# A transformer block on one core: which engine takes decays and normalisations, and how far a planner looks into its chains

## The chip, the core and the metric

One core of a Trainium2 chip. TensorE (PE) does matmuls and transposes, VectorE (DVE), ScalarE (ACT) and GpSimd (POOL) work on elements, SyncE (SP) issues DMAs. Each engine takes its instructions in the order in which the program has them. The metric is the device time of one launch in microseconds, the median of several executions. All data are float32; a matmul of the program stands in the trace as two MATMUL records, a transpose as one.

## The reference

Eight sequences (batches) of 512 tokens, width 256, go through one block of four residual steps:

```python
x = x + attn_a(layernorm(x))     # 16 heads of 16, keys and values through a latent of 64, rope,
                                 # softmax(q k / 4 + log decay(distance)) v, + 0.2 sigmoid(q mean k) mean v, Wo
x = x + ffn(layernorm(x))        # relu(x W1 + b1) W2 + b2, inner width 1024
x = x + attn_b(layernorm(x))     # (q k * gamma^(i-j) for i >= j) v, no softmax, one head of 256
x = x + ffn(layernorm(x))        # the same weights again
```

A layernorm is `(x - mean) / sqrt(var + 1e-5)` over 256 elements. The first attention's log decay is applied as a factor: `exp(score - max) * dec_a`, and the sum over keys comes out of the same matmul by a column of ones.

## The kernel before

**Items and steps.** The first attention is cut into 32 items (8 batches x 4 groups of 4 heads); each has 8 score tiles `s` (two heads, 128 queries x 512 keys each) and 8 probability tiles `t` (the same transposed). A step n of the planner issues on TensorE the four matmuls of `s_n` and `t_{n-12}`. `reduce_item` then takes the row maxima of `s` on VectorE (`mr`, TENSOR_REDUCE 128x1024); once an item's 8 are there, `shift` puts them, negated, into `qT` (`mx`, a transpose, an ACT copy and a DMA). `soft_item` makes `p` from `t`: Exp on ScalarE, then two multiplications with `dec_a` (the decays, TENSOR_TENSOR 128x512) on GpSimd or VectorE, as `pooled[n]` says. `pv_item` multiplies `p` with the values (`pv`).

**Banks.** `s` and `t` share two PSUM buffers of two banks (`ps_sc`), so `s_{n+1}` waits for the `mr` of `s_n`, and `t` for the Exp of the `t` before it. In early steps (`EARLY`) `t` may take two of the three single banks (`ps_m`), which everything else uses too; these tiles are named `t0_n`, `t1_n`.

**The other work.** Everything else is cut into `Unit`s in chains: `front1`/`front2` (layernorm `a`, latent `lat`, keys `k`, queries `q`, values `v`, gate `ga`, mean rows `mv`, `me`), `post_units` (division of the numerators by the sums), `rest(b)` (`wo`; layernorm `f`; feed-forward `hx2` and `x2`; layernorm `r`; second attention `b`, `bv`, `bs`, `bo`; layernorm `g`; feed-forward `hx4` and `x4`), and `rest_last` for the last batch, in two chains of half a batch. A name such as `hx2_7_0_1` is that unit's tile: batch 7, column block 0, second half.

**Layernorms.** `ln_units` makes three units for each half (two tiles of 128 tokens): `stats` (`st`, `mv` on VectorE; `ve`, the variance plus eps, and `rstd`, a power, on GpSimd), `norm` (`xn = (x - mean) * rstd`, two TENSOR_SCALAR 128x256 on VectorE; for `f` and `g` also two additions of the bias `b2` to `x` on GpSimd), and `turn` (four transposes `tr_`, then an ACT copy to `xT`).

**Division.** `post_units(i, fast)`: for groups 0 and 1, and for all groups of batches `fast` to 6, it goes by DMA: `num` copied out of PSUM, rows to `aT` and sums to `sums`, a reciprocal, a DMA to DRAM and a broadcast DMA back (`rec`), then `aT * rec` on VectorE. Otherwise groups 2 and 3 are transposed (`num`), divided, and turned back (`aT`). `wo` needs `aT`.

**The order.** All instructions are pinned to the order in which Python emits them. `plan(reserve, later, early, fast, lead, bias, emit)` walks through steps and chains with clocks of its own for PE, DVE, ACT and POOL. It runs once for each of 144 rules (lists `RESERVES` to `BIASES`) with `emit=False`; the rule with the least planned end is run again with `emit=True`. In its main loop, units without TensorE work (`pe` 0) are issued as soon as they are ready, but only from the head of a chain; the best TensorE unit at the head of a chain is taken if the next step must wait or if its credit allows; `values` issues `pv`.

```python
            prob_at[i] = clock["POOL" if pooled[i] else "DVE"] = on if pooled[i] else own
...
    cost = {r: plan(*r) for r in rules}
    plan(*min(rules, key=cost.get), emit=True)
```

In `step`, the matmuls, Exp and decays are emitted ahead of the lines that set `pooled[i]`; `soft_item` thus reads what an earlier call of `plan` left in `pooled`, that of the last rule in the list. The rule that this kernel's planner takes is (reserve 90000, later 0, early 8, fast 3, lead 3000, bias 3000), which is the last of the list.

Of the kernel before, what the change touches and what calls it, by code (L numbers as in the profile page):

```python
# [9 lines left out]
F32 = mybir.dt.float32  # L10
AF = mybir.ActivationFunctionType
ALU = mybir.AluOpType
# [23 lines left out]
def tile_kernel(  # L36
# [217 lines left out]
    RESERVES, LATERS, EARLIER, FAST = (75000, 90000), (-45000, -30000, 0), (0, 8), (1, 3)  # L254
    LEADS, BIASES = (0, 1500, 3000), (0, 3000)
    NS = 8 * NI
    LAG, FILL, BONUS = 12, 300, 300
    PER = 8 * NG
    EARLY = PER + 2
# [47 lines left out]
    class Unit:  # L307
        def __init__(self, fn, pe=0, then=(), after=(), step=0, gives=None, needs=(), bank=True):
            self.fn, self.pe, self.then, self.after, self.step = fn, pe, then, list(after), step
            self.gives, self.needs, self.banks, self.done = gives, needs, int(bank) if pe > 0 else 0, None  # L310
            self.takes = self.frees = False
            self.holds, self.lets, self.behind = [], [], []


# [13 lines left out]
    def ln_units(get, name, pool, bias=None):  # L328
        s = {}

        def stats(h):
            xt = get()
            if h == 0:
                s["st"] = rs.tile([P, NT, 6], F32, tag="st", name=f"st_{name}")
                s["mv"] = rs.tile([P, NT, 2], F32, tag="mv", name=f"mv_{name}")
                s["ve"] = rs.tile([P, NT], F32, tag="ve", name=f"ve_{name}")
                s["rstd"] = rs.tile([P, NT], F32, tag="rstd", name=f"rstd_{name}")
            two = slice(2 * h, 2 * h + 2)
            for t in (2 * h, 2 * h + 1):
                dve.bn_stats(s["st"][:, t, :], xt[:, t, :])  # L340
            for t in (2 * h, 2 * h + 1):
                dve.bn_aggr(s["mv"][:, t, :], s["st"][:, t, :])
            gps.tensor_scalar(s["ve"][:, two], s["mv"][:, two, 1], EPS, None, ALU.add)
            gps.tensor_tensor(s["rstd"][:, two], s["ve"][:, two], half[:, two], ALU.pow)

        def norm(h):
            xt = get()
            if h == 0:
                s["xn"] = rs.tile([P, NT, D], F32, tag="xn", name=f"xn_{name}")
                s["xT"] = pool.tile([P, NC, T], F32, tag="xT", bufs=1 if pool is fr else 2, name=f"xT_{name}")  # L350
            for t in (2 * h, 2 * h + 1):
                dve.tensor_scalar(
                    s["xn"][:, t, :], xt[:, t, :], s["mv"][:, t, 0:1], s["rstd"][:, t : t + 1],
                    ALU.subtract, ALU.mult,
                )
# [11 lines left out]
        u = []  # L367
        for h in range(2):
            a = Unit(lambda h=h: stats(h), then=(("DVE", 1200), ("POOL", 1450)))
            b = Unit(lambda h=h: norm(h), then=(("DVE", 1100),) + (() if bias is None else (("POOL", 1550, "aside"),)), after=[a])  # L370
            u.append([a, b, Unit(lambda h=h: turn(h), 520, (("ACT", 600),), after=[b])])
        Hold("st", 2, u[0][0], u[1][1]), Hold("xn", 2, u[0][1], u[1][2])
        return s, u

# [665 lines left out]
    def plan(reserve, later, early, fast, lead, bias, emit=False):  # L1040
# [26 lines left out]

        def issue(u):
            t = start_of(u)
            if emit:  # L1070
# [7 lines left out]
            for e, ns, *aside in u.then:  # L1078
# [85 lines left out]
        def step(t):  # L1164
# [11 lines left out]
            shape[0] = "S"  # L1176
            at_ += 1070
            clock["PE"] = at_
            if emit:
                mms, after = [], []  # L1180
                if s is not None:
                    ps, m = score_item(s)
                    mms += m
                    after.append((reduce_item, s, ps))
                for i in ts:
                    ps, m = prob_item(i)
                    mms += m
                    after.append((soft_item, i, ps))
                for o, l, r in mms:
                    mm(o, l, r)  # L1190
                for f, k, ps in after:
                    f(k, ps)
# [6 lines left out]
            for i in ts:  # L1199
                if spare[i]:  # L1200
                    for e in range(2):
                        clock["ACT"] = max(clock["ACT"], at_ + 100) + 650
                        banks.popleft()
                        banks.append(clock["ACT"])
                else:
                    clock["ACT"] = max(clock["ACT"], at_ + 100) + 1090
                    sc.popleft()
                    sc.append(clock["ACT"])

                on = max(clock["ACT"] + 60, clock["POOL"]) + 2750  # L1210
                own = max(clock["ACT"] + 60, clock["DVE"]) + (1650 if i < EARLY else 1500)
                pooled[i] = on <= own + (lead if i < EARLY else bias)
                prob_at[i] = clock["POOL" if pooled[i] else "DVE"] = on if pooled[i] else own

        def backlog():
# [48 lines left out]
        while t < LAST or any(chains) or posts or shifts or valued[0] < NS:  # L1264
            while True:
                ready = [
                    c for c in [shifts, posts] + chains
                    if c and not c[0].pe and c[0].step <= t and start_of(c[0]) is not None
                    and start_of(c[0]) <= clock["PE"] + 300
                ]  # L1270
                if not ready:
                    break
                for c in ready:
                    if start_of(c[0]) is not None:
                        issue(c.pop(0))
            s_step = step_start(t) if t < LAST else None

            idle = t >= LAST or s_step is None or s_step > clock["PE"] + 400
            free = t < 2 * PER or backlog() > reserve
            best = None  # L1280
            for rank, c in enumerate([shifts, posts] + chains):
                if not c or not c[0].pe or c[0].step > t:
# [4 lines left out]
                s = start_of(c[0])  # L1287
                if s is None:
                    continue

# [1 line left out]
                if t >= LAST:  # L1292
                    key = (max(s - (BONUS if c is last_two[0] or c is last_two[1] else 0), clock["PE"] + 50), -rank)
                if best is None or key < best[0]:
                    best = (key, c, s)


            full = t < LAST and steps[t][1] and steps[t][1][-1] - valued[0] >= PB
# [9 lines left out]
            elif one is not None and one <= soon and wait > FILL and not other:  # L1308
                k = 1
            if k and other and shape[0] == "S":  # L1310
                credit -= best[1][0].pe
                issue(best[1].pop(0))
                continue
            if k and (full or t < LAST or values_start(k) <= soon):
                values(k)
# [2 lines left out]
            if best is not None and not take:  # L1318
                soon = clock["PE"] + 50
                take = (best[1] is posts or best[1] is shifts or credit > 0) and best[2] <= max(soon, s_step)  # L1320
                take = take or idle and best[2] <= soon or best[2] + best[1][0].pe <= s_step
            if take and best is None:

                if valued[0] < NS:
# [7 lines left out]
                issue(c.pop(0))  # L1332
            elif take:
                if best[1] is not posts and best[1] is not shifts:
                    credit -= best[1][0].pe
                issue(best[1].pop(0))
            else:
                step(t)
                t += 1
# [118 lines left out]
```

## Time and profile before

| | |
|---|---|
| median of 3 runs | 1280.24 us (1279.64 to 1280.58) |
| the profiled execution | 1284.98 us; span from first to last instruction 1283.2 us |
| mean granted TensorE clock in it | 0.985 |
| VectorE: `mr`, 256 | busy 312.3 us, mean 1222 ns |
| VectorE: `xn_g` 28, `xn_f` 32, `xn_r` 32, `xn_a` 32 | 30.2, 29.3, 25.0, 20.4 us; mean 1118, 955, 820, 677 ns |
| GpSimd: `ve_f` 16 / `rstd_f` 16 (the others alike) | mean 250 ns / 736 ns |
| GpSimd: bias additions `x<-x,b` 60 | busy 45.1 us, mean 772 ns |
| ScalarE: `h_x` 128x512 with a few 128x256, 128 | minimum 474, median 687 ns |
| ScalarE: `rs<-rc` 128x512 from SBUF, 16 | median 621 ns |
| TensorE: `num` 32 / `aT` 16 transposes | busy 5.2 us / 2.5 us |

In the page, a busy time is the union of a group's instructions and the mean is that of one. "Idle before" is the time in which the engine stood still ahead of the group, with what ended it. In the windows view each stretch has its width, the busy time and number of instructions of PE, PEld (weight loads), DVE, ACT and POOL, the granted TensorE clock (1.00 is full), and the DMA share and rate. In the waits, three numbers follow a pair: total us, times, longest us. In the timeline a row begins with start and duration in us, and a bracket gives idle time before it and what ended it.

### The profile page before, as it was taken

The page shows a single profiled execution, that of the slowest core. Times are in us where ns is not written, and L with a number is a line of the kernel's source. Part 1 is how long each engine was busy: PE and PEld are TensorE (multiplying, and loading weights), DVE is VectorE, ACT ScalarE, POOL GpSimd, SP SyncE. Part 2 cuts the span into 40 slices and gives each one's busy share as a digit, 9 for nine tenths or more (in the row PEclk, how much of TensorE's full clock was granted, in tenths as well). Part 3 has the DMA queues.
Part 4 walks back from the last instruction along what each step waited for, and adds up shares of the span by engine and source line. Part 5 has one row for each costly group of instructions (what it writes and reads, how often), then busy time and mean ns, then how long its engine had stood idle before and what let it go on. Part 6 is the DMA issues. An engine that isn't in the chain of part 4 may idle for free.

```text
span 1283.2 us, 16000 instructions
## 1 busy us (share of the span) xinstructions
PE 1229.3 (96%) x6196; PEld 632.7 (49%) x6196; DVE 662.4 (52%) x989; ACT 464.3 (36%) x672; POOL 758.7 (59%) x747
## 2 busy tenths in 40 slices
PE   7988999989999999998999999999999999998997
PEld 5423345334535544354443644535543654376686
DVE  4667754775455675445644476435644364333121
ACT  2245443434353333432334234343334233512311
POOL 4379765777587675774667566675667465812000
PEclk9989999999999999998999999999999999998998
DMA  5401010001000100020000200011000100000000
GB/s 133 133 12 41 17 39 1 14 17 35 22 13 7 45 6 14 6 64 22 5 9 13 57 22 4 16 37 32 1 14 5 31 5 1 14 17 1 1 17 17
DMA packets 30872, 30.82 MB, mean 24 GB/s; under 512 B 12721, under 2 KB 22194, under 8 KB 30516
## 3 DMA queue, kind: packets, MB, share of 16 engines
q1 hardware_dynamic: 29884, 29.01, 8.3%
q8 instruction: 49, 0.80, 0.3%
q10 hardware_dynamic: 912, 0.79, 0.2%
q14 instruction: 27, 0.22, 0.1%
HBM read 13.39 MB, written 4.39 MB: 14 GB/s over the span
## 4 chain that ended last, share of the span: by engine, by line
PE 88%; DVE 7%; DMA 1%; issue 1%; POOL 1%; ACT 1%; SPq 0%; DVEq 0%; ACTq 0%
PE s L203 19%; PE x L203 18%; PE hx L203 18%; PE pv L203 8%; PE wo L203 3%; PE bs L203 3%; PE bo L203 3%; DVE mr L69 3%; PE b L203 2%; PE bv L203 2%; PE q L203 2%; PE t L203 2%; DMA wv_sb<-in_wv_dram 1%; PE warm L203 1%; PE lat L203 1%
## 5 line engine op out<-in xcount | busy, mean ns | idle before, releaser
L69 POOL TENSOR_TENSOR p<-p,dec_a 128x512 f32<-128x512 f32 x466 | 587.8, 1286 | 280.6 <-ACT p L69 280.3
L69 DVE TENSOR_REDUCE mr<-s 128x2 f32<-128x1024 f32 x256 | 312.3, 1222 | 288.1 <-PE t L203 266.6
L69 ACT ACTIVATE p<-t 128x1024 f32<-128x1024 f32 (+1 forms) x282 | 263.3, 945 | 417.8 <-PE t L203 407.6
L203 PE MATMUL s<-kT,qT 32*128 32x512 f32 x1024 | 291.8, 644 | 19.8 <-DVE mr L69 19.4
L203 PE MATMUL t<-qT,kT 32*128 32x512 f32 x1024 | 288.1, 644 | 1.6 <-DVE mv_a L69 1.6
L203 PE MATMUL x<-w_sb,h_x 128*128 128x256 f32 x960 | 221.6, 384 | 0.0
L203 PEld LDWEIGHTS x<-w_sb,h_x 128*128 128x128 f32 x960 | 178.0, 190 | 58.9 <-issue 33.6
L203 PEld LDWEIGHTS s<-kT,qT 32*128 32x128 f32 x1024 | 77.9, 184 | 161.8 <-DVE mr L69 68.6
L203 PE MATMUL pv<-p,va 128*32 128x512 f32 x1024 | 129.9, 608 | 0.0
L69 ACT ACTIVATE h_x<-hx,vec 128x512 f32<-128x512 f32 (+1 forms) x128 | 84.6, 661 | 120.3 <-PE hx L203 116.5
L203 PE MATMUL hx<-xT_g,w_sb 128*128 128x512 f32 (+1 forms) x288 | 124.6, 570 | 0.7 <-ACT xT_g L69 0.7
L203 PE MATMUL hx<-xT_f,w_sb 128*128 128x512 f32 (+1 forms) x288 | 123.2, 564 | 1.2 <-ACT xT_f L69 1.0
L69 DVE TENSOR_TENSOR x<-x,x 128x256 f32<-128x256 f32 x60 | 25.4, 424 | 164.6 <-PE x L203 159.6
L203 PEld LDWEIGHTS hx<-xT_g,w_sb 128*128 128x128 f32 x288 | 52.5, 195 | 66.3 <-issue 62.4
L203 PEld LDWEIGHTS t<-qT,kT 32*128 32x128 f32 x1024 | 77.8, 183 | 11.7 <-ACT p L69 3.9
L203 PEld LDWEIGHTS hx<-xT_f,w_sb 128*128 128x128 f32 x288 | 51.9, 194 | 60.1 <-issue 46.3
L69 POOL TENSOR_SCALAR ve_g<-mv_g 128x2 f32<-128x2 f32 x16 | 3.6, 226 | 101.6 <-DVE mv_g L69 101.6
L203 PEld LDWEIGHTS pv<-p,va 128*32 128x32 f32 x1024 | 25.0, 109 | 75.2 <-issue 54.5
L69 DVE TENSOR_TENSOR p<-p,dec_a 128x512 f32<-128x512 f32 x46 | 43.6, 985 | 19.3 <-ACT p L69 19.2
L69 POOL TENSOR_TENSOR x<-x,b 128x256 f32<-128x256 f32 x60 | 45.1, 772 | 6.6 <-DVE xn_g L69 4.6
L69 POOL TENSOR_TENSOR rc<-rc,rs 128x512 f32<-128x512 f32 x30 | 38.5, 1306 | 9.1 <-DVE rs L69 9.1
L203 PE MATMUL wo<-wo_sb,aT 128*128 128x256 f32 x128 | 36.5, 405 | 5.2 <-DVE aT L69 4.3
(164 smaller groups left out, 1126.1 us busy)
## 6 DMA issues: line engine op xcount, KB each, us to landing
kT<-rc SPq DMA_DIRECT2D x64, 64.0 KB
qT<-rc SPq DMA_DIRECT2D x60, 64.0 KB
x<-in_x_dram SPq DMA_DIRECT2D x7, 512.0 KB
out_dram<-x SPq DMA_DIRECT2D x28, 128.0 KB
aT<-num SPq DMA_DIRECT2D x96, 32.0 KB
rec<-d_rec SPq DMA_DIRECT2D x12, 256.0 KB
w_sb<-in_w_dram SPq DMA_DIRECT2D x2, 1024.0 KB
x<-in_x_dram SPq DMA_DIRECT2D x2, 256.0 KB
```

The source lines that it names most:

```text
L69: ins = f(*a, **k)
L203: tc.keep_in_program_order(nc.tensor.matmul(o, lhsT=l, rhs=r, start=start, stop=stop))
```

## The change

Four things are changed.

1. In `step`, the emission moves behind the lines that set `pooled[i]`, so that the decays are emitted on the engine that the same run of `plan` chose. The planned time of a pair of decays on VectorE is 2300 ns where GpSimd is busy for more than 300 ns beyond their start, and 1500 otherwise (before: 1650 early, 1500 later).
2. Units of layernorms (`stats` and `norm`) are marked `norm`. Those without TensorE work may be issued from any of the first `AHEAD = 6` places of a chain, and `product_of` finds a chain's first TensorE unit past marked ones.
3. `norm` runs on ScalarE (`on_act`: an activation Identity with scale `rstd` and bias `nm = -mean * rstd`, with `nm` a scalar_tensor_tensor 128x2 on VectorE) or on VectorE as before, by the planner's clocks when the unit is issued.
4. `ve` moves from GpSimd to VectorE; the planned times of `stats` and `norm` change; the second half's units of a layernorm stay behind the first half's (`behind`).

```diff
+    AHEAD = 6
...
-            gps.tensor_scalar(s["ve"][:, two], s["mv"][:, two, 1], EPS, None, ALU.add)
+            dve.tensor_scalar(s["ve"][:, two], s["mv"][:, two, 1], EPS, None, ALU.add)
...
+            if b[h].on_act:
+                dve.scalar_tensor_tensor(
+                    s["nm"][:, two], s["mv"][:, two, 0], -1.0, s["rstd"][:, two], ALU.mult, ALU.mult
+                )
             for t in (2 * h, 2 * h + 1):
...
+                if b[h].on_act:
+                    act.activation(
+                        s["xn"][:, t, :], xt[:, t, :], AF.Identity, bias=s["nm"][:, t : t + 1],
+                        scale=s["rstd"][:, t : t + 1],
+                    )
+                else:
+                    dve.tensor_scalar(
...
+            def choose(t, clock):
+                d = max(t, clock["DVE"])
+                slow = clock["POOL"] > d + 200
+                b[h].on_act = max(d + 300, clock["ACT"]) + 1300 < d + (2300 if slow else 1000)
+                return ((("DVE", 300), ("ACT", 1200)) if b[h].on_act else (("DVE", 2200 if slow else 1000),)) + more
...
-            a = Unit(lambda h=h: stats(h), then=(("DVE", 1200), ("POOL", 1450)))
-            b = Unit(lambda h=h: norm(h), then=(("DVE", 1100),) + (() if bias is None else (("POOL", 1550, "aside"),)), after=[a])
-            u.append([a, b, Unit(lambda h=h: turn(h), 520, (("ACT", 600),), after=[b])])
+            a = Unit(lambda h=h: stats(h), then=(("DVE", 1280), ("POOL", 950)))
+            b.append(Unit(lambda h=h: norm(h), then=normalised(h), after=[a]))
+            u.append([a, b[h], Unit(lambda h=h: turn(h), 520, (("ACT", 600),), after=[b[h]])])
+        for h in range(2):
+            u[h][0].norm = u[h][1].norm = True
+        for one, two in zip(*u):
+            two.behind.append(one)
...
-                own = max(clock["ACT"] + 60, clock["DVE"]) + (1650 if i < EARLY else 1500)
+                own = max(clock["ACT"] + 60, clock["DVE"])
+                own += 2300 if clock["POOL"] > own + 300 else 1500
                 pooled[i] = on <= own + (lead if i < EARLY else bias)
                 prob_at[i] = clock["POOL" if pooled[i] else "DVE"] = on if pooled[i] else own
+            if emit:
...
+                for f, k, ps in after:
+                    f(k, ps)
...
+        def product_of(c):
+
+            for u in c[:AHEAD]:
+                if u.pe:
+                    return u if u.step <= t else None
+                if not u.norm:
+                    return None
+            return None
...
                 ready = [
-                    c for c in [shifts, posts] + chains
-                    if c and not c[0].pe and c[0].step <= t and start_of(c[0]) is not None
-                    and start_of(c[0]) <= clock["PE"] + 300
+                    (c, u) for c in [shifts, posts] + chains for u in c[:AHEAD]
+                    if not u.pe and (u is c[0] or u.norm) and u.step <= t and start_of(u) is not None
+                    and start_of(u) <= clock["PE"] + 300
                 ]
```

The planner of the changed kernel takes the rule (reserve 90000, later 0, early 8, fast 1, lead 1500, bias 3000). In the two built programs these counts differ:

| engine, instruction | before | after |
|---|---|---|
| GpSimd / VectorE: half decays `p` | 466 / 46 | 482 / 30 |
| VectorE / ScalarE: `xn` | 128 / 0 | 52 / 76 |
| VectorE: `nm` | 0 | 38 |
| GpSimd / VectorE: `ve` | 64 / 0 | 0 / 64 |
| TensorE: transposes `num` / `aT` | 32 / 16 | 16 / 8 |
| TensorE: `warm` matmuls on the identity | 78 | 76 |
| SyncE: DMAs of the division (`aT`, `sums`, `d_rec`, `rec`) | 144 | 168 |

More of the change, by code (lines that the diff above doesn't have):

```diff
@@ L310, in __init__ @@
             self.gives, self.needs, self.banks, self.done = gives, needs, int(bank) if pe > 0 else 0, None
-            self.takes = self.frees = False
+            self.on_act = False
+            self.takes = self.frees = self.norm = False
             self.holds, self.lets, self.behind = [], [], []
@@ L337, in stats @@
                 s["rstd"] = rs.tile([P, NT], F32, tag="rstd", name=f"rstd_{name}")
+                s["nm"] = rs.tile([P, NT], F32, tag="nm", name=f"nm_{name}")
             two = slice(2 * h, 2 * h + 2)
@@ L350, in norm @@
                 s["xT"] = pool.tile([P, NC, T], F32, tag="xT", bufs=1 if pool is fr else 2, name=f"xT_{name}")
-            for t in (2 * h, 2 * h + 1):
[L352 to L355, printed above, removed]
+            two = slice(2 * h, 2 * h + 2)
+            if b[h].on_act:
+                dve.scalar_tensor_tensor(
+                    s["nm"][:, two], s["mv"][:, two, 0], -1.0, s["rstd"][:, two], ALU.mult, ALU.mult
+                )
+            for t in (2 * h, 2 * h + 1):
+                if b[h].on_act:
[5 more added lines that the diff above has]
+                    dve.tensor_scalar(
+                        s["xn"][:, t, :], xt[:, t, :], s["mv"][:, t, 0:1], s["rstd"][:, t : t + 1],
+                        ALU.subtract, ALU.mult,
+                    )
             if bias is not None:
@@ L365, in turn, with normalised @@
             act.copy(s["xT"][:, :, 2 * h * P : (2 * h + 2) * P], ps.rearrange("p (c t) -> p c t", c=NC))
-        u = []
-        for h in range(2):
-            a = Unit(lambda h=h: stats(h), then=(("DVE", 1200), ("POOL", 1450)))
-            b = Unit(lambda h=h: norm(h), then=(("DVE", 1100),) + (() if bias is None else (("POOL", 1550, "aside"),)), after=[a])
-            u.append([a, b, Unit(lambda h=h: turn(h), 520, (("ACT", 600),), after=[b])])
+        u, b = [], []
+        more = () if bias is None else (("POOL", 1550, "aside"),)
+        def normalised(h):
+            def choose(t, clock):
[3 more added lines that the diff above has]
+                return ((("DVE", 300), ("ACT", 1200)) if b[h].on_act else (("DVE", 2200 if slow else 1000),)) + more
+            return choose
+        for h in range(2):
+            a = Unit(lambda h=h: stats(h), then=(("DVE", 1280), ("POOL", 950)))
[5 more added lines that the diff above has]
+            two.behind.append(one)
         Hold("st", 2, u[0][0], u[1][1]), Hold("xn", 2, u[0][1], u[1][2])
@@ L1069, in issue @@
             t = start_of(u)
+            then = u.then(t + 100, clock) if callable(u.then) else u.then
             if emit:
@@ L1077, in issue @@
             t += 100
-            for e, ns, *aside in u.then:
+            for e, ns, *aside in then:
                 if e is None:
@@ L1178, in step @@
             clock["PE"] = at_
[L1179 to L1192, printed above, removed]
             if s is not None:
@@ L1210, in step @@
                 on = max(clock["ACT"] + 60, clock["POOL"]) + 2750
-                own = max(clock["ACT"] + 60, clock["DVE"]) + (1650 if i < EARLY else 1500)
+                own = max(clock["ACT"] + 60, clock["DVE"])
+                own += 2300 if clock["POOL"] > own + 300 else 1500
                 pooled[i] = on <= own + (lead if i < EARLY else bias)
                 prob_at[i] = clock["POOL" if pooled[i] else "DVE"] = on if pooled[i] else own
+            if emit:
+                mms, after = [], []
+                if s is not None:
+                    ps, m = score_item(s)
+                    mms += m
+                    after.append((reduce_item, s, ps))
+                for i in ts:
+                    ps, m = prob_item(i)
+                    mms += m
+                    after.append((soft_item, i, ps))
+                for o, l, r in mms:
+                    mm(o, l, r)
+                for f, k, ps in after:
+                    f(k, ps)
         def backlog():
@@ L1272, in plan @@
                     break
-                for c in ready:
-                    if start_of(c[0]) is not None:
-                        issue(c.pop(0))
+                for c, u in ready:
+                    if (u is c[0] or u.norm) and start_of(u) is not None:
+                        c.remove(u)
+                        issue(u)
             s_step = step_start(t) if t < LAST else None
@@ L1281, in plan @@
             for rank, c in enumerate([shifts, posts] + chains):
-                if not c or not c[0].pe or c[0].step > t:
+                u = product_of(c)
+                if u is None:
                     continue
@@ L1286, in plan @@
                     continue
-                s = start_of(c[0])
+                s = start_of(u)
                 if s is None:
@@ L1294, in plan @@
                 if best is None or key < best[0]:
-                    best = (key, c, s)
+                    best = (key, c, s, u)
             full = t < LAST and steps[t][1] and steps[t][1][-1] - valued[0] >= PB
@@ L1310, in plan @@
             if k and other and shape[0] == "S":
-                credit -= best[1][0].pe
-                issue(best[1].pop(0))
+                credit -= best[3].pe
+                best[1].remove(best[3])
+                issue(best[3])
                 continue
@@ L1320, in plan @@
                 take = (best[1] is posts or best[1] is shifts or credit > 0) and best[2] <= max(soon, s_step)
-                take = take or idle and best[2] <= soon or best[2] + best[1][0].pe <= s_step
+                take = take or idle and best[2] <= soon or best[2] + best[3].pe <= s_step
             if take and best is None:
@@ L1334, in plan @@
                 if best[1] is not posts and best[1] is not shifts:
-                    credit -= best[1][0].pe
-                issue(best[1].pop(0))
+                    credit -= best[3].pe
+                best[1].remove(best[3])
+                issue(best[3])
             else:
```

## The prediction

> **What bounds the kernel now.** I read the page's busy shares and chain first, then three stages in the windows view.
>
> ```profile
> PE 1229.3 (96%) x6196; PEld 632.7 (49%) x6196; DVE 662.4 (52%) x989; ACT 464.3 (36%) x672; POOL 758.7 (59%) x747
> ...
> PE 88%; DVE 7%; DMA 1%; issue 1%; POOL 1%; ACT 1%; SPq 0%; DVEq 0%; ACTq 0%
> ```
> ```profile
> 33.40:182.70 149.30, 137.47 (x759) 54.49 (x762) 109.22 (x138) 61.07 (x114) 106.21 (x99) 0.95 0.17 51
> 182.70:1157.80 975.10, 953.22 (x4806) 468.96 (x4800) 512.27 (x746) 367.07 (x484) 622.00 (x589) 1.00 0.07 18
> 1157.80:1280.20 122.40, 113.84 (x483) 91.25 (x482) 25.53 (x78) 27.25 (x53) 16.03 (x28) 0.94 0.03 8
> ```
> TensorE is the bound: the first figure after each width is its busy time. What can be won is its idle time, 11.8 us early (149.30 - 137.47), 21.9 us in the middle, 8.6 us in the tail, and what the granted clock (next to the 0.17, 0.07 and 0.03) costs. The mean clock of 0.985 is a loss of 19 us. Then I asked what TensorE waited for, and where.
>
> ```profile
> PE s L203 <- DVE mr L69: 19.4, 21, 2.0
> PE wo L203 <- DVE aT L69: 4.3, 2, 3.4
> ```
> ```profile
> 105.61 0.70 PE L203 MATMUL s<-kT,qT 32*128 32x512 f32 x2 [1.31 <-DVE mr L69]
> ...
> 583.42 1.22 PE L203 MATMUL wo<-wo_sb,aT 128*128 128x256 f32 x2 [3.40 <-DVE aT L69]
> ...
> 1164.35 0.78 PE L206 MATMUL tr_g<-ident,xn_g 128*128 128x128 f32 x4 [1.20 <-DVE xn_g L69]
> 1167.55 1.14 PE L206 MATMUL tr_f<-ident,xn_f 128*128 128x128 f32 x4 [2.42 <-DVE xn_f L69]
> ...
> 1261.85 1.23 PE L206 MATMUL tr_g<-ident,xn_g 128*128 128x128 f32 x4 [2.94 <-DVE xn_g L69]
> ```
> ```profile
> 582.28:589.11 6.83, 5.69 (x13) 4.54 (x14) 2.10 (x5) 0.00 (x0) 0.00 (x0) 0.50 0.00 0
> 1165.96:1172.79 6.83, 4.51 (x12) 3.43 (x13) 4.05 (x13) 1.06 (x2) 6.58 (x12) 0.50 0.00 0
> 1261.53:1268.36 6.83, 5.83 (x15) 4.39 (x16) 0.59 (x2) 1.54 (x3) 1.42 (x2) 0.50 0.00 0
> ```
> Each of the three long waits is followed by 6.83 us at clock 0.50, so each costs up to 3.4 us again.
>
> **The decays.** Nothing is repaired for the kernel before: the rule its planner takes is the last of its list, so the engines left by the last cost run are its own. The order of the built programs shows the new one taking its own rule with a lead of 1500: 482 half decays on GpSimd for 466, 30 on VectorE for 46.
>
> ```profile
> L69 POOL TENSOR_TENSOR p<-p,dec_a 128x512 f32<-128x512 f32 x466 | 587.8, 1286 | 280.6 <-ACT p L69 280.3
> ...
> L69 DVE TENSOR_TENSOR p<-p,dec_a 128x512 f32<-128x512 f32 x46 | 43.6, 985 | 19.3 <-ACT p L69 19.2
> ```
> GpSimd gets 16 x 1.286 = 21 us and loses 64 adds x 0.25 = 16 us: 759 becomes 764, no bound. VectorE loses 16 x 0.985 = 16 us.
>
> **The normalisations.** 76 of 128 `xn` go to ScalarE (the four large groups, 124 of them, are busy 105 us on VectorE, 0.85 each).
>
> ```profile
> L69 DVE TENSOR_SCALAR xn_f<-x,mv_f,rstd_f x32: 380/1118/1443, 169.5 to 1169.5; 128x256 f32<-128x256 f32 x32
> ...
> L69 DVE TENSOR_SCALAR ret<-ret,bb x7: 231/873/1346, 255.2 to 1148.4; 128x4 f32<-128x4 f32 x7
> ```
> The first row (minimum, median, maximum) is 0.4 us when GpSimd is quiet and 1.35 us beside it. The second is the nearest row for the moved add (128x2): 64 x 0.23 to 0.87 = 15 to 56 us; GpSimd works in 59% of the span, so I take 64 x (0.23 + 0.59 x 0.64) = 39. The new `nm` (38) lies between the 0.15 us of the 128x2 `mv_a` and the same 0.87; I take 0.15, the row of its own size and operation: 6 us. VectorE: -65 - 16 + 39 + 6 = -36 us of 662. On ScalarE an `xn` lies between 0.41 us (two thirds of the 0.621 us that a 128x512 from SBUF takes) and 0.475 us (128x256 `h_x`): 31 to 36 us on 464. Neither is the bound, and TensorE gains only where such a step ends its wait. Queued behind the new waits are: on VectorE, behind an `nm` that waits for `rstd`, the next `mr`, and behind that `s`; on ScalarE, behind an `xn` that waits for its `nm`, the Exp and evacuations, and behind them `t` and the banks. The old `xn` waited for `rstd` on VectorE in the same place, 3.2 + 1.5 + 0.9 = 5.6 us in all (the groups of `xn_f`, `xn_a`, `xn_r`), so `rstd` is mostly there in time, and I cost these waits within the small ones below. In waiting beside GpSimd alone, 76 x (0.85 - 0.41) = 33 us go and 64 x 0.59 x 0.64 = 24 us come.
>
> By the Trainium skill, SBUF — State Buffer, Who interferes with whom, a VectorE instruction with two SBUF inputs is shut out by a GpSimd one that reads SBUF: `nm`, which reads `mv` and `rstd`, would then wait too, where the `mv_a` row, with an input from PSUM, did not. No row has so small a one with both in SBUF; the second rival prices it.
>
> **Deeper look and new order.** With AHEAD = 6 a chain's statistics and normalisations may be issued before the work ahead of them. What came of it is read off the order of both programs and priced by rows.
>
> *Transposes.* The planner now takes FAST 1 for 3, so batches 1 and 2 divide by DMA in all groups: 16 `num` and 8 `aT` transposes go, at 5.2/32 and 2.5/16 us busy each: -3.8 us. SP gets 24 more issues; the waiter behind them is `wo`, next.
>
> *`wo` after the DMA division.* From the last `pv` of batches 3 to 6 to the end of the multiply the trace shows 28.2, 21.1, 21.8 and 23.8 us; in the old order 21 to 31 us of TensorE work lie between, and batches 3 and 6 paid 3.40 and 0.89 us. In the new order 25 to 41 us lie between (durations by block). I take no wait: -4.3 us, and -3.4 us for the half clock at 582. If the cover goes (batches 2 and 6 have 25 us), 3 us return each.
>
> *Steps back to back.* With no work between two steps the next `s` waits for `mr`. Of 15 such pairs the 6 whose `t` has its own banks paid 0.0, the 9 others 1.22 to 1.96 us, 12.4 in all. The new order has 6 of the dear kind (8.2 us) and 11 of the other: -4.2 us. Runs of three now stand early (steps 27 to 29, 41 to 43), where VectorE and GpSimd are busy 109 and 106 of 149 us, so I give the five added pairs half of 1.31: +3.3 us (0 to 6.5).
>
> *Tail.* The old order has only `wo` ahead of `tr_g6`, `tr_f7`, and nothing ahead of `tr_g7_1`: 0.24 + 1.20 + 2.42 + 0.73 + 0.24 + 2.94 + 0.68 = 8.45 us idle. The new one puts `tr_r6_1`, two `b_6` and `bv_6` (4.8 us) ahead of `tr_f7`, and six `hx4_6` (10 us) ahead of `tr_g7`; from the add to the first `xn` it takes 0.69 + 0.74 + 0.30 + 0.22 + 0.71 + 0.41 = 3.1 us, so both are hidden. New is `tr_r7`, behind `x2_7_3` with only the two `tr_g6` (0.9 us) ahead: on VectorE its first half's `nm` stands behind the last add and the second half's statistics, 0.42 + 1.4 + 0.15, then ScalarE's first `xn` 0.45 and hops of 0.1 to 0.2: 2.6 - 0.9 = 1.7 us, and 0.4 more till the second half's `xn`. New is also `aT_31`: behind `x2_6_3` VectorE does its add, two `xn` and the division, 0.42 + 0.82 + 0.25 + 0.43 = 1.9 us and hops, against 0.9 us of transposes: 1.2 us. With `wo`'s 0.24: -8.45 + 3.5 = -4.9 us.
>
> *Clock in the tail.* -2 x 3.4; half windows followed 1.6 to 2.6 us idle within some 3.4 us, and did not follow 1.3 to 1.7 us, so `tr_r7` makes one or none: +1.7. Another elsewhere: +1.7. Sum -3.4 us.
>
> The Trainium skill, TensorE: Matmul & The Clock Gate, Why this matters for your kernels, allows gaps up to about 3 us. Here 2.0 us idle in two pieces ahead of 1165.96 were enough, so the measurement decides. By the page the 1.7 us for `tr_r7` would drop out.
>
> *Small waits.* The middle keeps 21.9 - 7.8 (pairs) - 4.3 = 9.8 us of waits below 1.7 us. A new order draws them anew: a `pv` whose decays stand on GpSimd behind bias adds (1.5 us) and `rstd` (0.7 us) may be late, and on ScalarE an Exp now stands behind an `xn`. Between nothing and another 9.8 + 5 us, I give +6.
>
> **Sum.** -3.8 - 4.3 - 3.4 - 4.2 + 3.3 - 4.9 - 3.4 + 6 = -14.7; taken as -14. The profiled run took 1284.98 us (span 1283.2 and 1.8 around it), 4.7 us over the median of 1280.24; the difference carries over: 1266 us.
>
> **Rivals.** *Given back in the draw* (15%): the small waits cost 9 to 17 us and the early pairs their full 6.5. For: early, both helpers are some 72% busy. Against: the middle loses 2% of its time in all. -14 + 3..11 + 3: 1272 to 1280 us, at the middle 1276.
> *`nm` held* (8%): if each `nm` waits as the 128x4 row does, 38 x (0.87 - 0.23) = 24 us come on VectorE; with a third of them ahead of an `mr` that TensorE waits for, -14 + 8 = -6: 1274 us. Against: it needs GpSimd busy each time.
> *ScalarE's queue held* (14%), the other side: an `xn` there waits for `rstd`, behind a pair of decays on GpSimd (2.57 us); all Exp behind it wait, `t` keeps its buffer, TensorE stops. 38 halves x 2.57 = 98 us; -14 + 98 x share passes zero at one in seven; at one in four it is +10: 1290 us. Against: the 5.6 us above.
> *No effect of the choice* (inside the forecast): had `on_act` not been taken the order would still differ; 76 `xn` on ScalarE in the program rule it out.
> *More* (6%): few new waits, no half clock: -24, 1256 us.
>
> **Numbers.** Forecast 57% (1258 to 1272), more 6%, given back 15% (8 faster, 7 the same), `nm` 8%, queue 14%. Measurement of this kernel tells about 0.2%, 2.6 us. Faster 0.79, same 0.07, slower 0.14. The range 1256 to 1284 leaves out half of "more" and most of "queue".
>
> **What would show it.** Right: `tr_g7` and `wo` of all DMA batches without wait, no 0.50 window near 1160 and 1250 but at most one by `tr_r7`, six dear pairs, `num` x16, `xn` on ScalarE near 0.41 to 0.48 us, `ve` on VectorE between 0.23 and 0.9. Wrong: PE busy falls by 4 us but idle stays at 50; Exp behind `xn` with ScalarE idle for GpSimd's `rstd`; `pv` waiting for GpSimd's `p` by over 10 us.

## The result, and the profile after

| | before | after |
|---|---|---|
| median of 4 runs | 1280.41 us (1279.64 to 1284.29) | 1267.56 us (1266.34 to 1269.20) |
| the profiled execution, its span | 1284.98, 1283.2 | 1267.68, 1265.9 |
| mean granted clock in it | 0.985 | 0.995 |

The ratio is 0.9888 (0.9870 to 0.9907): 12.85 us less. The two profiled executions differ by 17.3 us, because that of before lies 4.6 us over its median and that of after 0.1.

The busy shares and the chain of the page after:

```profile
PE 1225.4 (97%) x6168; PEld 628.8 (50%) x6168; DVE 615.4 (49%) x995; ACT 499.4 (39%) x746; POOL 763.6 (60%) x699
...
PE 88%; DVE 6%; POOL 2%; DMA 2%; ACT 1%; issue 1%; SPq 0%; ACTq 0%; DVEq 0%
```

TensorE is still the bound. Its idle time, span less busy, is 1265.9 - 1225.4 = 40.5 us against 53.9. VectorE has lost 47 us, ScalarE has gained 35. The windows view by stage (width, then busy time and count of PE, PEld, DVE, ACT, POOL, granted clock, DMA share, rate):

```profile
32.43:180.50 148.07, 136.94 (x749) 55.80 (x749) 108.38 (x135) 62.00 (x118) 105.67 (x93) 0.99 0.17 51
180.50:1134.30 953.80, 937.79 (x4722) 454.51 (x4720) 459.07 (x733) 397.46 (x547) 629.02 (x556) 1.00 0.07 20
1134.30:1262.90 128.60, 125.83 (x547) 100.66 (x546) 32.44 (x97) 30.91 (x60) 14.81 (x21) 0.99 0.02 8
```

Idle is 11.1 us early (before 11.8), 16.0 in the middle (21.9) and 2.8 in the tail (8.6). The clock early is 0.99 for 0.95 and in the tail 0.99 for 0.94. TensorE's waits, with total, times and longest in us:

```profile
PE s L203 <- DVE mr L69: 17.0, 22, 2.1
...
PE s L203 <- ACT p L69: 2.4, 1, 2.4
PE tr_f L206 <- ACT xn_f L69: 2.4, 4, 1.2
PE tr_r L206 <- ACT xn_r L69: 1.6, 2, 1.4
...
PE wo L203 <- ACT aT L69: 0.2, 1, 0.2
```

The waits of `wo` for the division (`DVE aT`, 4.3 us) and of `tr_g` for `xn_g` are gone. The places in the timeline that answer to those shown of before:

```profile
98.69 0.70 PE L203 MATMUL s<-kT,qT 32*128 32x512 f32 x2 [1.31 <-DVE mr L69]
...
580.07 1.13 PE L203 MATMUL wo<-wo_sb,aT 128*128 128x256 f32 x4
...
1153.37 0.60 PE L206 MATMUL tr_f<-ident,xn_f 128*128 128x128 f32 x4
...
1187.42 0.33 PE L206 MATMUL tr_r<-ident,xn_r 128*128 128x128 f32 x1 [1.42 <-ACT xn_r L69]
...
1220.21 1.04 PE L206 MATMUL tr_g<-ident,xn_g 128*128 128x128 f32 x8
```

A pair of steps back to back still costs 1.31 us where the second `s` has to wait for `mr` (below, a dear pair; a cheap one is a pair whose `t` has banks of its own). `wo`, `tr_f` and `tr_g` start without a bracket, that is without a wait; `tr_r7` waits as forecast. One window of half clock follows it (the second line below). The first line follows a step that waited 2.1 us for `mr`; a wait of 2.4 us at 469.6 brought none. Of the three windows of 6.83 us that the prediction showed none is left:

```profile
1042.34:1045.75 3.41, 3.41 (x21) 1.01 (x13) 2.57 (x4) 2.00 (x3) 2.73 (x4) 0.50 0.00 0
1189.12:1192.54 3.42, 3.40 (x8) 2.78 (x9) 0.00 (x0) 0.93 (x2) 0.00 (x0) 0.51 0.00 0
```

All windows of half clock together are 37.6 us long before and 13.6 us after. The new and moved operations (minimum, median, maximum in ns, first and last start):

```profile
L69 ACT ACTIVATE xn_f<-x,nm_f,rstd_f x28: 585/593/612, 176.0 to 1144.1; 128x256 f32<-128x256 f32 x28
...
L69 DVE SCALAR_TENSOR_TENSOR nm_f<-mv_f,rstd_f x14: 146/152/1221, 175.8 to 1142.4; 128x2 f32<-128x2 f32 x14
```
```profile
L69 DVE TENSOR_SCALAR ve_f<-mv_f x16: 168/374/1237, 172.4 to 1142.3; 128x2 f32<-128x2 f32 x16
```
```profile
L69 POOL TENSOR_TENSOR p<-p,dec_a 128x512 f32<-128x512 f32 x482 | 610.0, 1290 | 296.5 <-ACT p L69 290.1
...
L69 DVE TENSOR_TENSOR p<-p,dec_a 128x512 f32<-128x512 f32 x30 | 35.7, 1227 | 18.1 <-ACT p L69 18.1
```

An `xn` on ScalarE takes 593 ns whatever runs beside it; the two small ones on VectorE vary by a factor of seven or eight.

### The profile page after: what moved, and what is told of

Its sections match the earlier page's. It is cut to its first block, busy times and chain, and to the rows that moved or that the text cites. A ratio compares the mean times of both kernels' runs of the same rounds, so it can differ in the third digit from the quotient of the medians.

```text
span 1265.9 us, 15939 instructions
## 1 busy us (share of the span) xinstructions
PE 1225.4 (97%) x6168; PEld 628.8 (50%) x6168; DVE 615.4 (49%) x995; ACT 499.4 (39%) x746; POOL 763.6 (60%) x699
## 4 chain that ended last, share of the span: by engine, by line
PE 88%; DVE 6%; POOL 2%; DMA 2%; ACT 1%; issue 1%; SPq 0%; ACTq 0%; DVEq 0%
PE hx L203 19%; PE s L203 18%; PE x L203 18%; PE pv L203 8%; PE wo L203 3%; PE bs L203 3%; PE bo L203 3%; DVE mr L69 3%; PE b L203 2%; PE bv L203 2%; PE q L203 2%; POOL p L69 2%; PE t L203 2%; PE warm L203 1%; PE lat L203 1%; PE ga L203 1%
## 5 line engine op out<-in xcount | busy, mean ns | idle before, releaser
L69 POOL TENSOR_TENSOR p<-p,dec_a 128x512 f32<-128x512 f32 x482 | 610.0, 1290 | 296.5 <-ACT p L69 290.1
L203 PE MATMUL pv<-p,va 128*32 128x512 f32 x1024 | 132.8, 608 | 1.6 <-ACT num L69 0.7
L203 PE MATMUL hx<-xT_g,w_sb 128*128 128x512 f32 (+1 forms) x288 | 122.0, 560 | 0.0
L203 PEld LDWEIGHTS t<-qT,kT 32*128 32x128 f32 x1024 | 78.6, 183 | 14.2 <-ACT p L69 5.4
L69 POOL TENSOR_TENSOR x<-x,b 128x256 f32<-128x256 f32 x60 | 43.9, 754 | 14.7 <-DVE xn_g L69 11.6
L69 DVE TENSOR_TENSOR p<-p,dec_a 128x512 f32<-128x512 f32 x30 | 35.7, 1227 | 18.1 <-ACT p L69 18.1
L69 POOL TENSOR_TENSOR rstd_g<-ve_g,half 128x2 f32<-128x2 f32 x16 | 11.3, 704 | 54.0 <-DVE ve_g L69 53.8
L69 ACT COPY num<-pv 128x512 f32<-128x512 f32 x32 | 18.7, 585 | 57.9 <-PE pv L203 53.4
```

Source lines behind the costliest of these rows:

```text
L69: ins = f(*a, **k)
L203: tc.keep_in_program_order(nc.tensor.matmul(o, lhsT=l, rhs=r, start=start, stop=stop))
```

## Experiments

Two theories stood first. **O**: the order of the work alone makes the gain, as the prediction has it, and which engine makes an `xn` matters little. **E**: VectorE's relief makes a good part of it, because the steps' row maxima `mr`, for which TensorE waits most, no longer stand behind an `xn` in VectorE's queue. In the table, ratios are to the kernel before, run beside each version on the same chip (its medians there: 1281.96 us for c1 to c4, 1284.63 for c5 to c8, 1283.21 for c9 to c11 and 1282.12 for c12); idle is span less TensorE's busy time, "half" the length of all half-clock windows, both of the profiled execution.

| run | median us | ratio (interval) | idle | half |
|---|---|---|---|---|
| c1_after_again | 1268.30 | 0.9891 (0.9872 to 0.9910) | 39.4 | 17.1 |
| c2_norm_dve | 1283.99 | 1.0017 (1.0006 to 1.0028) | 53.4 | 20.5 |
| c3_tail_no_ahead | 1273.94 | 0.9937 (0.9919 to 0.9954) | 45.8 | 13.7 |
| c4_before_ahead | 1277.88 | 0.9965 (0.9950 to 0.9981) | 52.1 | 17.1 |
| c5_before_norm_act | 1287.60 | 1.0025 (1.0010 to 1.0040) | 55.7 | 30.7 |
| c6_extra_dve | 1290.74 | 1.0053 (1.0036 to 1.0071) | 53.6 | 34.1 |
| c7_ve_pool | 1269.09 | 0.9887 (0.9868 to 0.9906) | 41.2 | 17.1 |
| c8_ahead1 | 1287.20 | 1.0023 (1.0012 to 1.0034) | 51.8 | 23.9 |
| c9_before_tail_ahead | 1281.82 | 0.9987 (0.9973 to 1.0000) | 51.6 | 34.1 |
| c10_all_act_held | 1275.45 | 0.9939 (0.9919 to 0.9960) | 42.8 | 30.7 |
| c11_wide_rules | 1277.16 | 0.9963 (0.9944 to 0.9982) | 39.8 | 27.3 |
| c12_tail_kept | 1270.68 | 0.9915 (0.9895 to 0.9935) | 42.1 | 10.2 |

**The changed kernel again**, unaltered, as the measure for the others.

> The changed kernel once more, on the chip of the next three, to have its time and clock with a narrower interval: 1266 to 1269 us. Both theories expect the same. If the granted clock differs from run to run by 0.005, the time should differ by about half of 0.005 x 1266 = 3 us, since a half-clock window costs half of its length.

Measured: 1268.30 us, the ratio of the first comparison within its interval.

**The new order without the relief.** The choice is still made for the planner's clock, so the order stays, but every `xn` is emitted on VectorE and no `nm`.

```diff
-            if b[h].on_act:
+            on_act = False
+            if on_act:
                 dve.scalar_tensor_tensor(
...
-                if b[h].on_act:
+                if on_act:
                     act.activation(
```

> The order of the changed kernel is kept instruction for instruction, but the 76 xn that stood on ScalarE stand on VectorE, and the 38 nm go. Theory O (the gain comes from the order of TensorE's work): VectorE has TensorE's work between its steps as cover, so 0 to +3 us over the changed kernel. Rival E (the gain comes from the relief of VectorE): VectorE gets 76 x 0.85 - 38 x 0.39 = 50 us back, and a quarter of that lies ahead of an mr that TensorE waits for: +8 to +13 us, that is, back to the time before.

Measured: 1283.99 us, 15.7 us over c1_after_again and no better than before. O falls in its plain form. TensorE's waits, first of c1_after_again, then of c2_norm_dve:

```profile
PE s L203 <- DVE mr L69: 15.2, 20, 2.1
...
PE mx L206 <- DVE mr L69: 0.6, 2, 0.3
...
PE t L203 <- DVE mr L69: 0.2, 1, 0.2
```
```profile
PE s L203 <- DVE mr L69: 20.7, 23, 2.5
...
PE t L203 <- DVE mr L69: 4.3, 2, 2.7
...
PE hx L203 <- DVE me L69: 2.3, 1, 2.3
...
PE mx L206 <- DVE mr L69: 1.9, 3, 1.3
```

Waits for `mr` rise from 16.0 to 26.9 us, and `me`, another VectorE result, is newly late: together 13.2 us more, where idle grows by 14.0. The waits for `xn` add some 4 us, and one of 2.4 us for an Exp goes. One place shows how. In the changed kernel the second `s` of a dear pair near 593 us waits 1.32 us, the time of one `mr`. Here two `xn` stand ahead of that `mr` in VectorE's queue, and the same `s` waits 2.50 us:

```profile
606.17 2.70 DVE L69 TENSOR_SCALAR xn_f<-x,mv_f,rstd_f 128x256 f32<-128x256 f32 x2
608.80 1.21 DVE L69 TENSOR_REDUCE mr<-s 128x2 f32<-128x1024 f32 x1
...
610.07 0.70 PE L203 MATMUL s<-kT,qT 32*128 32x512 f32 x2 [2.50 <-DVE mr L69]
```

What the order had won on TensorE is still there in this run: `wo` waits 0.2 us, the tail's waits are 2.6 us (3.1 in the changed kernel), no window of half clock comes after 496 us, and the six dear pairs stand idle for 10.2 us (9.0). It is paid back in other places.

**Look-ahead out of the tail.** The rule is fixed to the changed kernel's own, and behind the last step chains show only their head.

```diff
-            for u in c[:AHEAD]:
+            for u in c[: AHEAD if t < LAST else 1]:
```

> The changed kernel with its own rule, but after the last step the look into a chain is one unit deep; up to there the order is the same. tr_f7 then has only tr_r6_0 (0.45 us) between it and wo_7, and tr_r7_0 only tr_g6_0. Theory O: tail idle grows from 3.1 to 5 to 7 us, with one half-clock window more (1.7): +3 to +6 us. Rival E: the tail has no steps and VectorE is idle 75% of it, so 0 to +1 us. tr_g7 keeps six hx4_6 ahead of it in this order, so its 2.9 us should not come back by either.

Measured: +5.6 us on c1_after_again, O's 3 to 6. The waits name the place (2.5 us in c1_after_again; the one of 4.3 us stands in the tail):

```profile
PE tr_f L206 <- ACT xn_f L69: 7.9, 7, 4.3
```

**Look-ahead alone.** The kernel before with `AHEAD` and `product_of`, planned anew; `xn` on VectorE, `ve` on GpSimd, its old prices, the decays on the engines of its own plan.

> The kernel before with the deeper look alone: layernorm units may be issued from the first six places of a chain; xn stays on VectorE, ve on GpSimd, all planned times as before, and the decays stand on the engines of the run's own plan. The order has 5 dear pairs and 9 cheap ones, and the tail has tr_r6_1, two b_6 and hx4_6 as cover. Theory O: most of the gain, 1266 to 1272 us. Rival E: little, 1276 to 1281 us.

Measured: -4.1 us, a third of the gain. Its order has 5 dear pairs for 9 and in the tail no wait over 0.8 us, but VectorE is late in new places:

```profile
PE s L203 <- DVE mr L69: 22.0, 28, 2.0
PE t L203 <- DVE mv_a L69: 4.7, 1, 4.7
PE mx L206 <- DVE mr L69: 4.6, 5, 1.4
PE tr_a L206 <- DVE xn_a L69: 4.0, 6, 0.9
```

**The relief alone.** The old order is held, and the same 76 `xn` go to ScalarE.

```diff
+            on_act = f"{name}.{h}" in ON_ACT
+            if on_act:
+                dve.scalar_tensor_tensor(
+                    s["nm"][:, two], s["mv"][:, two, 0], -1.0, s["rstd"][:, two], ALU.mult, ALU.mult
+                )
             for t in (2 * h, 2 * h + 1):
+                if on_act:
+                    act.activation(
...
```

> The kernel before in its own order, to the instruction on TensorE, with one edit: the 76 normalisations (xn) that the changed kernel gives to ScalarE are given to ScalarE here too, each pair behind one small VectorE instruction (nm). ve stays on GpSimd. Theory R (a relief of VectorE pays by itself: the steps' row maxima, mr, no longer stand behind an xn in VectorE's queue; in the new order it was worth 15.7 us, of which the waits for mr, 16.0 against 26.9 us, are 10.9): 1266 to 1273 us, ratio 0.988 to 0.993, and the trace's waits for mr fall by 7 us or more from those of the kernel before. Theory B (both are needed: the old order was planned with the xn on VectorE and has room for them, so that the relief meets no wait there): 1276 to 1283 us, ratio 0.996 to 1.001. Theory L (the xn on ScalarE comes later by 0.3 to 0.6 us for the nm and its hand-over, and the old order has no look-ahead to cover that): slower than before, above 1284 us, with waits tr <- ACT xn above 5 us.

Measured: ratio 1.0025, slower by a little and just above B's range; B, with something of L. VectorE is busy 617.9 us for 662.4 and TensorE gains nothing:

```profile
PE s L203 <- DVE mr L69: 17.3, 20, 2.0
...
PE tr_g L206 <- DVE xn_g L69: 4.6, 3, 2.9
PE wo L203 <- DVE aT L69: 4.3, 2, 3.4
PE tr_f L206 <- ACT xn_f L69: 3.0, 3, 2.7
```

The large waits of the old order stand where they stood. Those of `s` for `mr` fall by 2.1 us (19.4 to 17.3), and all waits for an `xn` together rise from 9.5 to 14.2. A dear pair waits for the 1.2 us of `mr` itself, `wo` for a DMA division, the tail for a chain with nothing ahead of it; a shorter queue on VectorE helps none of these.

So there are four corners: old order, `xn` on VectorE 1; old order, ScalarE 1.0025; new order, VectorE 1.0017; new order, ScalarE 0.989. Added up, the two moves would give 1.004. The gain is all in their meeting. (The new order has `ve` on VectorE in both its corners; c7_ve_pool below shows what that is worth. The decays moved by change 1 were not tried by themselves; c8_ahead1 has them together with changes 3 and 4 and gains nothing.)

**VectorE's queue by itself.** The changed kernel with two reads of a constant behind each of the 76 `xn` that ScalarE makes; nobody uses what they write.

```diff
+                    dve.bn_stats(spent, wv_sb)
+                    dve.bn_stats(spent, wv_sb)
```

> The changed kernel in its own order, with two instructions more on VectorE behind each of the 76 nm's pairs: bn_stats of 128x256 elements of a constant into a tile that nobody reads (two for each xn that ScalarE makes; the trace has 0.413 us for one, so 76 x 2 x 0.413 = 63 us of VectorE's time, about what the 76 xn took there in c2_norm_dve). No result depends on them; they only stand in VectorE's queue where the xn stood. Theory Q (what the relief saved was the queue: mr and me behind xn): 1277 to 1286 us, with waits for mr near 25 us as in c2_norm_dve. Theory X (what it saved was the xn's own finish, made earlier on ScalarE): 1267 to 1271 us, waits for mr near 16 us as in the changed kernel.

Measured: 1290.74 us, a ratio of 1.0053 to before where the changed kernel has 0.989, some 21 us; Q. The load was 64.6 us, and waits for `mr` come back (24.8 us with those of `mx`, for 16.0):

```profile
L69 DVE BATCH_NORM_STATS2 spent<-wv_sb 128x6 f32<-128x256 f32 x152 | 64.6, 425 | 3.9
```
```profile
PE s L204 <- DVE mr L69: 22.1, 24, 2.7
...
PE t L204 <- DVE mr L69: 2.1, 2, 1.9
PE hx L204 <- DVE me L69: 1.5, 1, 1.5
```

At the place shown for c2_norm_dve four of the reads now stand ahead of the `mr`, and the `s` waits 2.74 us:

```profile
607.06 1.80 DVE L69 BATCH_NORM_STATS2 spent<-wv_sb 128x6 f32<-128x256 f32 x4
...
610.04 1.22 PE L204 MATMUL s<-kT,qT 32*128 32x512 f32 x2 [2.74 <-DVE mr L69]
```

The reads feed nothing: what came later came later by standing behind them.

**`ve` back on GpSimd**, in the changed kernel's order.

```diff
-            dve.tensor_scalar(s["ve"][:, two], s["mv"][:, two, 1], EPS, None, ALU.add)
+            gps.tensor_scalar(s["ve"][:, two], s["mv"][:, two, 1], EPS, None, ALU.add)
```

> The changed kernel in its own order with the 64 instructions ve (128x2, variance plus epsilon) back on GpSimd, where each took 0.25 us in the trace of before; on VectorE they took 0.25 to 0.49 us in the changed kernel, 20.7 us together. Theory Q (VectorE's queue is what counts): 20.7 us of 615 off VectorE, at the rate of 15.7 us for 57, is -5 us: 1262 to 1266 us, if the 64 times 0.25 us on GpSimd cost nothing. Theory H (the hand-over between two engines counts, one more on the way to each rstd): 1268 to 1273 us, with more waits for xn. No effect: 1266.5 to 1270 us, which the prediction's step (ve at a small price, hidden) would give.

Measured: no effect, 0.9887 for 0.9891. VectorE is 16 us less busy, but the waits for `mr` are 16.0 us as in the changed kernel, so Q at a constant rate is wrong: where in the queue the time stands decides.

**The engine choice without look-ahead**: `AHEAD = 1`, planned anew.

> The changed kernel with the depth of look-ahead 1 in place of 6, planned anew: a chain shows only its first unit, as in the kernel before, while the engine of each xn is chosen by the clock (82 on ScalarE) and ve is on VectorE. Its order has 9 dear and 6 cheap pairs of steps back to back, as the kernel before has, against 6 and 11. Theory R (relief by itself, the look-ahead being worth only its 4 us: 1281.96 less 1277.88): 1268 to 1273 us. Theory B (both needed): 1276 to 1282 us. In either, the tail should show waits tr <- xn of some 5 us more than the changed kernel's 1.6 (7.9 in c3_tail_no_ahead).

Measured: ratio 1.0023, above B's range but B by its waits. VectorE is busy only 602.0 us, yet the order has 9 dear pairs again, and the old waits are there:

```profile
PE s L203 <- DVE mr L69: 25.5, 28, 2.6
PE tr_f L206 <- ACT xn_f L69: 4.9, 5, 4.3
...
PE wo L203 <- DVE aT L69: 3.2, 2, 1.9
PE tr_g L206 <- DVE xn_g L69: 2.8, 1, 2.8
```

**The tail's look-ahead alone**, in the kernel before with its rule fixed: the look-ahead applies only where `t >= LAST`.

> The kernel before with its own rule and order for the 256 steps, and the look-ahead only behind the last step: there the row chains show the statistics and normalisations that stand behind a product. 9 dear and 6 cheap pairs, 128 xn on VectorE and 46 decays on VectorE as before; only the tail differs. Theory T (the tail is a term of its own, worth the 5.6 us that taking the look-ahead out of the changed kernel's tail cost): 5 us below before, ratio 0.995 to 0.997, with the waits tr_f <- xn_f (2.4 us) and hx (0.7) gone and one window of half clock less; the last wait tr_g <- xn_g (2.9 us) stays, because nothing stands ahead of it here either. Theory B (no part pays without the relief of VectorE): within 1.5 us of before, since an xn on VectorE ahead of its time stands before a ret or another xn.

Measured: -1.4 us, at the edge of what can be told, so nearer to B. `tr_f7` no longer waits its 2.4 us, but now the second half of `tr_g6` does, 0.96 us behind the 1.20 of the first, and a window of 6.83 us follows as before:

```profile
1165.59 0.78 PE L206 MATMUL tr_g<-ident,xn_g 128*128 128x128 f32 x4 [1.20 <-DVE xn_g L69]
1167.33 1.13 PE L206 MATMUL tr_g<-ident,xn_g 128*128 128x128 f32 x4 [0.96 <-DVE xn_g L69]
```

**All 128 `xn` on ScalarE**, in the changed kernel's order (`on_act = True` at emission).

> The changed kernel in its own order with the other 52 normalisations on ScalarE too (128 of 128), each pair behind its nm on VectorE. VectorE loses about 28 us of xn and gains 26 nm, some 6 us: 22 us less. Theory Q at a constant rate (15.7 us for 57 us, c2_norm_dve): -6 us, 1261 to 1265 us. Theory P (the planner has given each xn to the engine on which it is early enough, so what is left on VectorE stands in nobody's way): 1266.5 to 1270 us. Theory S (nm, hand-over and a ScalarE queue that now has p and xT behind xn): 1271 to 1278 us, with waits for ACT xn and ACT p above the 4.1 and 3.2 us of the changed kernel.

Measured: 0.9939, some 6 us worse than the changed kernel, though VectorE is 21 us less busy; S. Waits for `mr` stay at 15, those for ScalarE's `xn` rise from 4.1 to 9.7 us:

```profile
PE tr_f L206 <- ACT xn_f L69: 4.4, 6, 1.9
PE tr_r L206 <- ACT xn_r L69: 3.7, 5, 1.4
...
PE tr_g L206 <- ACT xn_g L69: 1.6, 3, 1.3
```

In the tail, where GpSimd rests, VectorE's `xn` was the quicker one (its shortest 0.41 us, without `nm` and hand-over, against 0.593). In its profiled execution, 3.9 us over the median, idle grows by 3.4 us and the half-clock windows by 13.6, which cost about half of that; the clock is the larger part of it.

**Wider rules.** Longer lists for the planner.

```diff
-    RESERVES, ..., FAST = (75000, 90000), ..., (1, 3)
-    LEADS, BIASES = (0, 1500, 3000), (0, 3000)
+    RESERVES, ..., FAST = (75000, 90000, 105000), ..., (1, 2, 3)
+    LEADS, BIASES = (0, 750, 1500, 2250, 3000), (1500, 3000, 4500)
```

> The changed kernel with a wider list of rules to choose from (RESERVES to 105000, FAST also 2, LEADS every 750, BIASES to 4500), so that another order is taken: 2 dear and 11 cheap pairs of steps back to back against 6 and 11, 80 xn on ScalarE, 20 decays on VectorE against 30, but the transposes of num in 32 pieces instead of 16. By the prediction's terms: 4 dear pairs less at 1.3 to 1.4 us each (-5.4), num's pieces +2.0 us, 10 decays off VectorE 12 us x 0.27 = -3: 1261 to 1265 us. Rival: the dear pairs come back as waits for mr in other places, or as steps above 1.2 us: 1266 to 1272 us.

Measured: 0.9963, worse than the rival's range. The planner's least end is not the chip's. Waits of `s` for `mr` fall to 10.2 us as the pairs say, and idle is that of c1_after_again, but two waits in the tail that the changed kernel lacks bring 10 us of half clock with them:

```profile
PE tr_g L206 <- ACT xn_g L69: 3.2, 1, 3.2
PE tr_g L206 <- DVE xn_g L69: 2.8, 1, 2.8
```

**Fewer dear pairs with the tail kept**: the rule fixed to one with 4 dear pairs and nearly the changed kernel's tail.

> The changed kernel with the planner's rule fixed to (90000, -15000, 8, 1, 1500, 4500): 4 dear and 11 cheap pairs against 6 and 11, num in 16 pieces as in the changed kernel, 78 xn on ScalarE, 26 decays on VectorE against 30, and, unlike c11_wide_rules, behind the last step nearly the changed kernel's order (tr_r6 stands one product earlier, one hx one place later). Theory T (c11_wide_rules lost in its tail, 3.2 and 2.8 us of waits with their half clock, what it gained on dear pairs): two dear pairs less, -2.7 us, and the tail's waits as in the changed kernel: ratio to before 0.985 to 0.988 (the changed kernel 0.989), waits for mr 13 us or less. Theory D (dear pairs come back elsewhere, whichever the tail): ratio 0.989 to 0.994, waits for mr 15 us or more, or others in their place.

Measured: 0.9915 (0.9895 to 0.9935); D. The tail is good, but a `tr_r` that starts at 414 has waited 3.3 us, and `wo` waits 3.7 us in four places. No version here is clearly faster than the changed kernel.

## Why the prediction was right, and where it was not

Time and sign came out, 1267.56 us for 1266, and so did the places in the order that the prediction named; one condition behind them did not. Term by term, in the pair of profiled executions (medians differ less, see above):

| term | predicted | measured |
|---|---|---|
| transposes, `num` 5.2 to 2.6 and `aT` 2.5 to 1.3 | -3.8 | -3.8 |
| `wo` after the DMA division | -4.3 | -4.3 |
| dear pairs (6 left, 9.0 us for 12.4) | -4.2 | -3.4 |
| cheap pairs (11 for 6) | +3.3 | +1.3 |
| tail, idle (8.45 to 3.13) | -4.9 | -5.3 |
| clock, at 582, in the tail and elsewhere | -6.8 | -9.7 |
| small waits | +6 | +3.7 |
| the remainder: other TensorE work longer | 0 | +4.2 |
| sum | -14.7 | -17.3 |

- *Decays.* Count and GpSimd's 764 us are met. VectorE's 30 took 1227 ns each for the 985 taken: it saved 43.6 - 35.7 = 8 us, not 16.
- *Normalisations.* The bounds of the `xn` on ScalarE, 0.41 to 0.475 us, missed: 0.593. The two rows they came from, a 128x512 copy from SBUF and an `h_x`, were of another kind. `ve` was taken too dear (20.7 us in all for 39), `nm` too cheap (14.5 for 6): 25 of the 38 `nm` take 0.14 to 0.16 us, and 13 take 0.33 to 1.22, each of which ends 0.01 to 0.02 us after the GpSimd instruction that was running when it began. These 13 agree with the rule from the Trainium skill, SBUF — State Buffer, Who interferes with whom, which the prediction weighed. The rival made of it 24 us on VectorE, a third of them on the path; it was 38 times 0.38 us in all, on average 0.23 over the quiet value, or 9 us. The 52 `xn` left on VectorE average 0.62 us for the 0.85 of before; in all VectorE fell by 47 us for the forecast 36. ScalarE's queue was held only once, when an Exp stood behind an `xn` and TensorE waited 2.4 us.
- *The step that failed* is a statement behind the sum: that TensorE gains from the engines' relief only where such a step ends its wait, so that the relief was priced at nothing and the order's terms stood by themselves. It is true of the old order (c5_before_norm_act). In the new one it is false by 15.7 us (c2_norm_dve): the terms for `wo` and the tail are there without the relief and that for the pairs nearly so, but the same order then stands idle for 14.0 us more, most of it before an `mr` or `me` that is late on VectorE. The +6 us for small waits thus held only with the relief, which the sum does not say. The prediction's remark that without the choice the order would still differ, and so bring its gain, falls with it. The time came out because the kernel has both; that the sum needed no term for the relief was luck.
- *Cheap pairs.* That the old ones paid 0.0 was read from idle time. By the timeline, a step takes TensorE 1.06 us from its `s` to the next product; in the kernel before, six steps that follow such a `t` take over 1.2 us, 4.4 us in excess together. The wait is inside the step, where the waits of TensorE's matmuls do not show it. After, nine of them have 5.1 us in excess and 0.56 of idle. One of these begins at 109.92 us and takes 2.16 us; in the timeline the weight load for the second half of its `t` waits 0.64 us for an Exp.
- *Tail.* Its sum hid two misses. The 1.2 us for `aT_31` did not come, and 1.3 us that it did not name did: 0.9 for `xT_r` and 0.4 for the `xn` of `tr_r6`.
- *Small waits.* Idle time not accounted for above fell by 1.0 us, and 10 other steps are above 1.2 us for 4 of before, by 6.2 us in excess for 1.5: +3.7.
- *Clock.* Half of TensorE's busy time inside the windows is 16.5 us before and 6.8 after. The rule on gaps (the Trainium skill, TensorE: Matmul & The Clock Gate, Why this matters for your kernels) would have left `tr_r7` without a window; 1.42 and 0.16 us idle were followed by one of 3.41 us, as the rows had it.
- *What was not seen* is that the same products take longer in the new order: `pv` +2.8 us, `b` +1.2, `bv` +1.1 and `v` +0.7 at full clock, with some others a little shorter. What makes them longer was not tried.
- *The carry-over.* That the median would fall by as much as the profiled execution was wrong: the 4.6 us by which the profile of before lay above its median, mostly half clock, did not carry over. A sum too small by 2.6 us and this made up for one another in part.

In the old order TensorE stood for reasons that VectorE's load hardly touches (c5). In the new one most of these are gone, and where an `xn` stands ahead of the next `mr`, its time in VectorE's queue becomes time of the kernel (c2, c6). This account fits c4 and c8 too. Why the old order has room for the `xn` and the new one has not is argued from the waits, and why the remaining `xn`, `ve` and decays on VectorE should cost nothing (c7, c10) only from their places.

## What to carry to other kernels

Test both halves of a change that moves work between engines and also reorders it: here each alone brought nothing or a third, and together 1.1%. An engine at 50% sets the pace wherever the bound engine's next step is queued behind its side work, so price a relief by who stands behind it in the queue, in the order that will run and not in the one profiled. And look for waits inside a step's own duration too, not only in idle time.

## What the runs showed of the hardware

- Half clock is drawn anew in each execution. In 18 executions of the kernel before, beside c1_after_again, the time goes with the mean clock: six at 0.989 have a median of 1280.53 us, seven at 0.988 1282.44, three at 0.985 1285.66.
- A normalisation of 128x256 with two pointers takes ScalarE 583 to 621 ns in all these runs, steady beside GpSimd; VectorE needed from 380 ns for the same, and a mean of 1118 in its dearest group (`xn_g` of the kernel before).
- An instruction of 128x2 on VectorE can take 1.2 us beside GpSimd: in the changed kernel `nm` 0.14 to 1.22, `ve` 0.17 to 1.24. Of the 64 `ve`, which have one input in SBUF, 41 take over 0.2 us, each begun while a GpSimd instruction ran; the 21 begun while GpSimd was quiet take 0.17.
